# When the sums of exponentials, the roundings and the totals are issued in an attention stage with heads of 64

## The chip, the cores and the metric

The kernel runs on one core of one Trainium2 chip. The metric is the device time of one execution in microseconds (us); the time given for a kernel is the median of its runs. The core has engines that run side by side, each through its own instructions in a fixed order: PE (matrix products), DVE (vector), ACT (scalar functions), POOL (a second, slower vector engine) and SP, which here only issues DMAs. An instruction that waits holds back everything behind it on its own engine.

## The reference, cut to what matters

The program is a chain of twelve layers on a sequence of 2048 tokens of width 128: four groups, each of a feed-forward layer, an attention and the feed-forward layer again. The change touches the last attention alone (16 heads of 64, rotary embedding, causal):

```
q = rope(x @ wq.T)                      # 16 heads of 64
latent = x @ w_kv_down.T                # 64 wide
k, v = rope(latent @ w_k_up.T), latent @ w_v_up.T
scores = q @ k.T / sqrt(64) + causal
probs = softmax(scores)                 # float32
x = x + (probs @ v, heads joined) @ wo.T
```

## The kernel before

One Python function records the twelve stages. A scheduler then orders the recorded instructions on each engine: PE instructions wrapped in `pe(...)` keep the order in which they were recorded; on DVE, ACT, POOL and SP an instruction is placed when, by the scheduler's own model, its inputs are ready and its engine is free, and the recorded order decides between those that are ready together.

The last attention works on pairs of heads (64 rows of PE each, so that two matmuls run side by side) and on blocks of 512 queries: 8 pairs times 4 blocks make 32 items. `flash` records two streams that are interleaved by a planned share of columns.

- Stream A (`stream_a`) computes rough scores with queries on the rows (line 1069) and their row maxima on DVE (`mp`, line 1087, 294 of them in the stage). The maxima of an item become a third operand of the exact scores (`put_max`, lines 1959 to 1972).
- Stream B (`stream_b`) goes through an item in units: one unit is 128 keys by up to 512 queries for both heads. It records the exact scores (line 1167, eight matmuls, plus a mask at line 1020 on the diagonal), the two exponentials (ACT, line 1175, out tile `pt`) and, directly behind each exponential, `on_exp`. Then the unit is handed over as `pend`, and its value products (`values()`, line 1132) are recorded after the scores and exponentials of the next unit. `pt` has six buffers, two per unit.
- `on_exp` (line 1993) adds the exponentials into `sum`, one tile for each head. The first unit of an item is kept and added together with the second (or copied at line 1984 where the item has only diagonal units). Additions alternate between DVE and POOL; the last two units of an item are on DVE.
- `finish` runs after an item's last value product. It plans a chain with the planner's clock (`after(delay, ...)`, in ns of PE columns): `total` (column sums on PE, line 2006, copied by ACT at line 2010, sent by DMA at lines 2014 and 2016), `inverse` (reciprocal, line 2026, DMAs at 2027 and 2029), `scaled` (`ov` at line 2036), `out_b` (output product at line 2042, added to `x` on DVE at line 2045).
- Beside both streams, `fill` issues pieces of the projections of later items. `half` computes one half of a rotated query or key block (PE lines 227 to 229 or 1736 and 1737; DVE line 1772, tile `rot`), `whole` adds the halves on POOL (line 1782), and `high`, which is put into `timed` to be called LATER ns on, rounds the sum to a high part on ACT (`h`, line 1787), takes the low part on POOL (line 1788) and sends both to DRAM (lines 1789 and 1790). `rot0` has two buffers. Line 1841 loads queries and keys back, up to four items ahead.

The small PSUM tiles `s2` (three buffers) are shared by the exact scores and by `rot`, `pm`, `sums`, `py` and `v`; a score matmul can start only when an earlier user of its bank has been read.

Of the kernel before, what the change touches and what calls it, by code (L numbers as in the profile page):

```python
# [64 lines left out]
def tile_macaron(ctx: ExitStack, tc: tile.TileContext, a: dict, out: bass.AP, stages=STAGES):  # L65
# [591 lines left out]
    LATER = ((0, -60, -200, -300), (0, -40, -80, -120))  # L657
# [312 lines left out]
    def flash(io, pool, early, its, nh, causal, scale, s1, s2, pv_mm, put_max, begin, finish, poll=None,  # L970
              on_exp=None, split_at=1, fill=None, leads=None, hook=None, flush=True, order=None):
# [5 lines left out]
        halved = nh == 2  # L977
        clock = [0.0]
        total = [0]
# [13 lines left out]
        def pe(ins):  # L993
            return tc.keep_in_program_order(ins)
# [109 lines left out]
        def stream_b():  # L1104
            pend = [None]

            def values(half=None):

                if pend[0] is None:
                    return  # L1110
                n, kt, nt, c0, pts, pv, last_exp = pend[0]

                whole = not tiled or kt == 0 or CH - c0 <= CH // 2
                if half is None:
                    lo, hi = (c0 if pend_half[0] == 0 else CH // 2), CH
                elif whole:
                    lo, hi = (c0, CH) if half == 0 else (CH, CH)
                else:
                    lo, hi = (c0, CH // 2) if half == 0 else (CH // 2, CH)
                pend_half[0] = 0  # L1120
                if half == 0:
                    pend_half[0] = 1
                    if hi == CH:
                        pend[0] = None
                        pend_half[0] = 0
                else:
                    pend[0] = None
                for j in reversed(range(nh)):
                    if lo == hi:
                        break  # L1130
                    lhsT, out_rows = pv_mm(n, j, kt)
                    i = pe(nc.tensor.matmul(  # L1132
                        pv[out_rows, lo:hi], lhsT, pts[j][:, lo:hi], start=kt == 0, stop=kt == nt - 1 and hi == CH
                    ))
                    if j == nh - 1:

                        tc.add_manual_dep(
                            i.ins, last_exp.ins.name,
                            mybir.DependencyInfo(
                                mybir.DependencyClass.Sync, mybir.DependencyReason.DATA  # L1140
                            ),
                            reason="together",
                        )
                step((hi - lo) * 4)
                if kt == nt - 1 and hi == CH:
                    finish(n, pv, after, pe)

            pend_half = [0]

            for n, (g, qc) in enumerate(its):  # L1150
                while n not in ready:
                    yield 0
                at[0], at[1] = n, 0
                nt = chunks(qc) * TC
                pv = None
                for kt in range(nt):
                    at[1] = kt
                    c0 = CH - width(kt, qc)
                    diag = causal and kt >= qc * TC
                    pts = {}  # L1160
                    if halved:
                        outs = [bank("s2"), bank("s2")]
                        terms = [s2(n, j, kt) for j in range(2)]
                        for i in range(len(terms[0])):
                            for j in range(2):
                                lhsT, rhs = terms[j][i]
                                pe(nc.tensor.matmul(  # L1167
                                    outs[j][:, c0:], lhsT, rhs[:, c0:],
                                    start=i == 0, stop=i == len(terms[0]) - 1 and not diag,
                                ))  # L1170
                        if diag:
                            half_masks([ps[:, c0 : c0 + P] for ps in outs], "maskk")
                        for j in range(2):
                            pts[j] = early.tile([P, CH], F32, name="pt", tag="pt", bufs=2 * nh + 2)
                            ex = nc.scalar.activation(pts[j][:, c0:], outs[j][:, c0:], AF.Exp, scale=scale)  # L1175
                            if on_exp is not None:
                                on_exp(n, kt, j, pts, c0)
                        step((CH - c0) * (len(terms[0]) - 2))
                        yield 2 * (CH - c0)
                        values()  # L1180
                    for at_j, j in enumerate(() if halved else order):
                        if alive[0] or at_j % 2:
                            ps = bank("s2")
                        else:
                            ps = first_pass_bank()[:, :CH]
                        terms = s2(n, j, kt)
                        for i, (lhsT, rhs) in enumerate(terms):
                            pe(nc.tensor.matmul(  # L1188
                                ps[:, c0:], lhsT, rhs[:, c0:],
                                start=i == 0, stop=i == len(terms) - 1 and (tiled or not diag),  # L1190
                            ))
                        if diag and not tiled:
                            pe(nc.tensor.matmul(
                                ps[:, c0 : c0 + P], masks_b["ident_b"], masks_b["maskk_b"], start=False, stop=True
                            ))
                        pt = early.tile([P, CH], F32, name="pt", tag="pt", bufs=2 * nh + 2)
                        ex = nc.scalar.activation(pt[:, c0:], ps[:, c0:], AF.Exp, scale=scale)  # L1197
                        if diag and tiled:
                            ex = nc.gpsimd.affine_select(
                                pt[:, c0 : c0 + P], pt[:, c0 : c0 + P], [[1, P]], ALU.is_ge, 0.0,  # L1200
                                base=0, channel_multiplier=-1,
                            )
                        pts[j] = pt
                        if on_exp is not None:
                            on_exp(n, kt, j, pts, c0)
                        if len(terms) > 1:
                            step((CH - c0) * (len(terms) - 1))
                        yield CH - c0
                        if tiled and alive[0]:
                            if at_j % 2:  # L1210
                                values(at_j // 2)
                        elif at_j == (split_at if alive[0] else nh - 1):
                            values()
                    if pv is None:
                        pv = held("pv")
                    pend[0] = (n, kt, nt, c0, pts, pv, ex)
                    if not alive[0]:
                        io.lead(2.3)
                if poll is not None:
                    at[1] = nt  # L1220
                    if flush and n + 1 < len(its) and its[n + 1][0] != g:
                        values()
                    poll(at)
            values()
# [475 lines left out]
    def attn3(io, k, w, early):  # L1700
        D = L3D
        NP = L3H // 2
        NK, NQ, NV = 6, 5, 5
        SPACE, AHEAD, LATER, SHARE = 1300.0, 12, 3500.0, 2
        RC, OUT = 5000.0, 8000.0
        wdn, raw = w
        xT, lat = [None] * NC, [None] * NC
# [42 lines left out]
        pieces, pieces_v, timed = [], [], []  # L1750
# [3 lines left out]
        def make(m):  # L1754
            p, c = its[m]
            halves = {}

            def half(what, i):
                if what == "q" and i == 0:
                    halves["tabs"] = tabs_of.pop()  # L1760
                    if c == 0:
                        weights(p)
                wh, wl = pw[p]
                o = (2 * (what == "k") + i) * P
                w = tuple(t[:, o : o + P] for t in (wh, wl))
                ps = bank("rot")
                if what == "q":
                    product(ps, w, xT[c])
                else:
                    latents(ps, w, lat[c], False)  # L1770
                t = scratch(F32R, f"rot{i}")
                nc.vector.tensor_tensor(t.bitcast(F32), ps, halves["tabs"][i], ALU.mult)  # L1772
                halves[i] = t
                if i == 1:
                    if what == "k":
                        tabs_of.append(tables(scratch, "l3rope", (c + 1) % NC))
                    whole(what)
# [36 lines left out]
        with tc.tile_pool(name="att0", bufs=1) as pool0, tc.tile_pool(name="att", bufs=1) as pool:  # L1814
# [182 lines left out]
            def finish(n, pv, after, pe):  # L1997
# [41 lines left out]
                def out_b():  # L2039
# [6 lines left out]
                    if p == NP - 1:  # L2046
                        io.mark(qc)

                after(2500.0, total)

            flash(io, pool, pool, its, 2, True, 0.125, s1, s2, pv_mm, put_max, begin, finish, watch,
                  on_exp, split_at=1, fill=fill, leads=leads)
# [241 lines left out]
```

## Time and profile before

| what | value |
|---|---|
| median of 3 runs | 3780.92 us (3779.64 to 3800.57) |
| the profiled execution's own time | 3787.8 us |
| its span, first to last instruction | 3786.1 us |
| stretch of the last attention | about 2700 to 3640 us of the span |
| PE busy in the span | 3471.8 us |
| additions of exponentials in the stage (line 1993), DVE | 338 |
| the same on POOL | 218 |
| roundings in the stage (line 1787, ACT) | 52, 619 ns each |
| totals in the stage (line 2006, PE) | 124 records, 612 ns each |

The profile comes from one execution. "Busy" is the union of an engine's instruction records; the records of PE overlap, since matmuls are pipelined and pairs run side by side. "A <- B" in a list of waits says that engine and line A sat idle until B was done.

### The profile page before, as it was taken

The numbers are of one execution on the slowest core, as the hardware profiler recorded it, in microseconds if no ns is written. First come the engines' busy times: TensorE is split into PE (matmuls) and PEld (weight loads), VectorE is DVE, ScalarE is ACT, GpSimd is POOL, SyncE is SP. The second block draws the span as 40 slices with busy tenths as digits, with TensorE's granted clock in tenths as the row PEclk, the third lists the DMA queues.
The fourth block names the chain that finished last, engine by engine and source line by source line (L and its number), as shares of the span: only waits on it lengthen the run. The fifth ranks groups of instructions, "written<-read, shape, count | busy, mean of one in ns | idle before, by whom it ended". The sixth has DMA issues, their size and how long they took to land. (4 is left out here: it accounts for less than half of the span.)

```text
span 3786.1 us, 64819 instructions
## 1 busy us (share of the span) xinstructions
PE 3471.8 (92%) x25405; PEld 1858.4 (49%) x25405; DVE 2866.0 (76%) x4795; ACT 2049.4 (54%) x3858; POOL 833.8 (22%) x834
## 2 busy tenths in 40 slices
PE   7689988979999999996999999988899999999989
PEld 5543356853333333783333333366444444445457
DVE  6588556667999997668799999654767776777862
ACT  3246822315888888322688888732334444444442
POOL 1511123010000000112000000142555444533341
PEclk9779989975999999996799999899899999999999
DMA  3410123000000000102000000012443232211010
GB/s 104 94 50 17 39 60 88 1 26 5 14 10 14 8 3 1 35 1 70 8 15 6 16 6 4 7 53 75 149 140 113 92 108 96 92 63 49 24 34 12
DMA packets 124115, 170.47 MB, mean 45 GB/s; under 512 B 24032, under 2 KB 51938, under 8 KB 123808
## 3 DMA queue, kind: packets, MB, share of 16 engines
q1 hardware_dynamic: 121248, 161.07, 13.6%
q0 software_dynamic: 2560, 5.25, 0.9%
q8 instruction: 200, 3.28, 0.4%
q14 instruction: 107, 0.88, 0.1%
HBM read 101.51 MB, written 45.87 MB: 39 GB/s over the span
## 5 line engine op out<-in xcount | busy, mean ns | idle before, releaser
L1087 DVE TENSOR_REDUCE mp<-s 128x2 f32<-128x1024 f32 (+3 forms) x1440 | 1628.5, 1183 | 111.6 <-PE s L1069 69.6
L1197 ACT ACTIVATE pt<-s 128x512 f32<-128x512 f32 (+1 forms) x2368 | 1220.9, 602 | 256.7 <-PE s L1188 157.7
L1132 PE MATMUL pv<-pt,v 128*32 128x256 f32 (+5 forms) x9848 | 1068.6, 445 | 23.0 <-ACT ov L1566 10.9
L1188 PE MATMUL s<-q,km 32*128 32x512 f32 (+2 forms) x2368 | 753.3, 508 | 23.5 <-ACT pt L1197 13.7
L1069 PE MATMUL s<-km,qt 32*128 32x512 f32 (+3 forms) x2368 | 638.4, 522 | 57.3 <-DVE mp L1087 35.9
L1188 PEld LDWEIGHTS s<-q,km 32*128 32x128 f32 (+1 forms) x2368 | 330.4, 190 | 553.2 <-issue 358.8
L1175 ACT ACTIVATE pt<-s 128x512 f32<-128x512 f32 (+3 forms) x640 | 306.1, 530 | 381.9 <-PE s L1167 237.8
L1132 PEld LDWEIGHTS pv<-pt,v 128*32 128x32 f32 (+1 forms) x9848 | 236.1, 113 | 401.2 <-issue 208.0
L143 POOL TENSOR_TENSOR rs<-rs,minus_half 128x4 f32<-128x4 f32 x56 | 57.4, 1025 | 1562.1 <-DVE rs L142 1561.3
L1993 DVE TENSOR_TENSOR sum<-sum,pt 128x512 f32<-128x512 f32 (+3 forms) x328 | 260.4, 811 | 104.9 <-ACT pt L1175 103.0
L1993 POOL TENSOR_TENSOR sum<-sum,pt 128x512 f32<-128x512 f32 (+1 forms) x200 | 268.2, 1341 | 208.0 <-ACT pt L1175 204.7
L1167 PE MATMUL s<-q,k 64*128 64x512 f32 (+3 forms) x1920 | 299.5, 404 | 14.7 <-ACT pt L1175 9.8
L1069 PEld LDWEIGHTS s<-km,qt 32*128 32x128 f32 (+1 forms) x2368 | 242.5, 196 | 119.4 <-DVE mp L1087 79.2
L1167 PEld LDWEIGHTS s<-q,k 64*128 64x128 f32 x1920 | 161.8, 188 | 209.1 <-issue 122.1
L715 ACT ACTIVATE sg<-pg 128x1024 f32<-128x1024 f32 x72 | 73.9, 1027 | 174.3 <-PE pg L229 158.8
L1069 PE MATMUL s<-k,q 64*128 64x512 f32 (+3 forms) x640 | 135.0, 434 | 13.1 <-DVE mp L1087 12.3
L725 PEld LDWEIGHTS pd<-l1d,h 128*128 128x128 f32 x1152 | 139.3, 192 | 5.6
L725 PE MATMUL pd<-l1d,h 128*128 128x128 f32 x1152 | 140.1, 275 | 0.0
L1772 DVE TENSOR_TENSOR rot<-rot,tab 128x512 f32<-128x512 f32 x128 | 87.7, 686 | 62.5 <-PE rot L229 32.0
L717 DVE TENSOR_TENSOR h<-pu,sg 128x1024 f32<-128x1024 f32 x72 | 87.9, 1221 | 60.5 <-PE pu L229 55.4
L1167 PE MATMUL s<-q,two 64*128 64x512 f32 (+3 forms) x640 | 128.8, 370 | 0.0
L1782 POOL TENSOR_TENSOR rot<-rot,rot 128x512 f32<-128x512 f32 x64 | 88.6, 1385 | 160.5 <-DVE rot L1772 125.7
(573 smaller groups left out, 4585.7 us busy)
## 6 DMA issues: line engine op xcount, KB each, us to landing
tab<-in_l3rope SPq DMA_DIRECT2D x66, 256.0 KB
q<-q SPq DMA_DIRECT2D x32, 512.0 KB
k<-k SPq DMA_DIRECT2D x32, 512.0 KB
l0e<-in_l0e SPq DMA_DIRECT2D x32, 256.0 KB
q<-h SPq DMA_DIRECT2D x32, 256.0 KB
q<-rot SPq DMA_DIRECT2D x32, 256.0 KB
k<-h SPq DMA_DIRECT2D x32, 256.0 KB
k<-rot SPq DMA_DIRECT2D x32, 256.0 KB
```

The lines of the kernel that those rows point to most:

```text
L717: nc.vector.tensor_tensor(h.rearrange("p m n -> p (m n)"), pu, sg, ALU.mult)
L725: nc.tensor.matmul(pd[:, i, :], h[:, m, i * P : (i + 1) * P], wd[:, m, :], start=m == 0, stop=m == 1,)
L1069: pe(nc.tensor.matmul(ps[:, o : o + w], lhsT, rhs[:, :w], start=True, stop=not masked))
L1087: ins = nc.vector.tensor_reduce(mp[:, r, j0 : j0 + 2, kc], both[:, :, :w], AX.X, ALU.max,)
L1132: i = pe(nc.tensor.matmul(pv[out_rows, lo:hi], lhsT, pts[j][:, lo:hi], start=kt == 0, stop=kt == nt - 1 and hi == CH))
L1167: pe(nc.tensor.matmul(outs[j][:, c0:], lhsT, rhs[:, c0:], start=i == 0, stop=i == len(terms[0]) - 1 and not diag,))
L1175: ex = nc.scalar.activation(pts[j][:, c0:], outs[j][:, c0:], AF.Exp, scale=scale)
L1188: pe(nc.tensor.matmul(ps[:, c0:], lhsT, rhs[:, c0:], start=i == 0, stop=i == len(terms) - 1 and (tiled or not diag),))
L1197: ex = nc.scalar.activation(pt[:, c0:], ps[:, c0:], AF.Exp, scale=scale)
L1772: nc.vector.tensor_tensor(t.bitcast(F32), ps, halves["tabs"][i], ALU.mult)
L1782: nc.gpsimd.tensor_tensor(f, f, halves[1].bitcast(F32), ALU.add)
L1993: eng.tensor_tensor(t[:, c0:], other[:, c0:], pts[j][:, c0:], ALU.add)
```

## The change

Three things are altered, all for the attention with heads of 64.

The two `on_exp` calls of a unit leave the place directly behind its exponentials and are recorded at the head of `values()`, ahead of the unit's value products. They thus come after the scores and exponentials of the next unit. `high` is planned 9000 ns after `whole` instead of 3500, and `half` now calls waiting `high`s first when more than one is waiting at the start of a new rotated tile. `total` is planned 4000 ns after an item's last value product instead of 2500.

```diff
@@ values(), in stream_b
                 n, kt, nt, c0, pts, pv, last_exp = pend[0]
+                if halved:
+
+                    for j in range(2):
+                        on_exp(n, kt, j, pts, c0)
@@ stream_b
                             ex = nc.scalar.activation(pts[j][:, c0:], outs[j][:, c0:], AF.Exp, scale=scale)
-                            if on_exp is not None:
-                                on_exp(n, kt, j, pts, c0)
                         step((CH - c0) * (len(terms[0]) - 2))
@@ attn3
-        SPACE, AHEAD, LATER, SHARE = 1300.0, 12, 3500.0, 2
+        SPACE, AHEAD, LATER, SHARE = 1300.0, 12, 9000.0, 2
@@ make(m)
             def half(what, i):
+                while i == 0 and len(timed) > 1:
+                    timed.pop(0)[1]()
@@ finish
-                after(2500.0, total)
+                after(4000.0, total)
```

No instruction is added or removed.

## The prediction

> **What bounds the kernel now.** I read the page first: engine shares, the busy tenths and the chain.
>
> ```profile
> PE 3471.8 (92%) x25405; PEld 1858.4 (49%) x25405; DVE 2866.0 (76%) x4795; ACT 2049.4 (54%) x3858; POOL 833.8 (22%) x834
> ...
> PE   7689988979999999996999999988899999999989
> ...
> PE 13%; DVE 2%; issue 1%; DMA 1%; POOL 1%; ACT 0%; SPq 0%; POOLq 0%; ACTq 0%; DVEq 0%
> PE s L1167 4%; PE pv L1132 3%; PE s L1069 1%; PE bank L228 1%; PE bank L229 1%; PE bank L227 1%; DVE mp L1087 1%; PE py L2042 0%; PE s L1020 0%; PE bank L922 0%; DVE sum L1993 0%; ACT pt L1175 0%; PE sums L2006 0%; DMA sum<-inv 0%; DMA inv<-rc 0%
> ```
>
> PE is at 9 tenths nearly everywhere, and the chain runs mostly through PE. The change touches only the stage from about 2700 to 3640 us, so the second view is busy time by stretch (stretch, length, busy time per engine with instruction counts, granted clock, DMA share, GB/s):
>
> ```profile
> 2700.00:3640.00 940.00, 899.57 (x6070) 449.20 (x6070) 711.39 (x1033) 402.50 (x812) 444.36 (x334) 0.98 0.26 85
> ```
>
> PE is idle for 940.0 - 899.6 = 40.4 us there. Third, the waits of that stretch (us in total, times, longest): of PE, then of DVE and of ACT.
>
> ```profile
> PE s L1167 <- ACT pt L1175: 9.8, 9, 2.0
> PE s L1069 <- DVE mp L1087: 9.7, 16, 1.3
> PE pm L1967 <- DVE rot L1772: 5.6, 4, 2.9
> PE rot L229 <- POOL pwL L222: 3.6, 2, 2.8
> PE s L1167 <- DVE x L2045: 3.1, 3, 1.8
> ...
> PE sums L2006 <- DVE rot L1772: 1.2, 3, 0.4
> PE sums L2006 <- DVE sum L1993: 0.9, 1, 0.9
> ```
>
> ```profile
> DVE sum L1993 <- ACT pt L1175: 105.3, 104, 3.4
> ```
>
> ```profile
> ACT h L1787 <- POOL rot L1782: 114.1, 51, 4.4
> ```
>
> The two queues that the change aims at do stall (105 us in DVE behind an addition that waits for its exponential, 114 us in ACT behind a rounding that waits for POOL), but PE sees little of it: 9.7 us for maxima, 9.8 us for exponentials. Those stalls lie beside PE work. Fourth, one stretch of the timeline, to see such a stall reach PE:
>
> ```profile
> 3133.97 1.27 POOL L1993 TENSOR_TENSOR sum<-sum,pt 128x512 f32<-128x512 f32 x1 [3.04 <-ACT pt L1175]
> 3134.35 1.44 DVE L1993 TENSOR_TENSOR sum<-sum,pt 128x512 f32<-128x512 f32 x1
> ...
> 3135.71 1.21 DVE L1087 TENSOR_REDUCE mp<-s 128x2 f32<-128x1024 f32 x1
> ...
> 3136.98 0.50 PE L1069 MATMUL s<-k,q 64*128 64x512 f32 x2 [0.57 <-DVE mp L1087]
> ```
>
> The maximum starts when the addition ends, and PE waits 0.57 us for its bank.
>
> **The change part by part.** No work is added, so the cost is all in order. I compared the order of the built programs engine by engine, which the diff alone does not tell. Nothing differs ahead of the last attention. In it, the scheduler had already placed most instructions when their inputs are ready, so few move.
>
> *Additions a unit on.* Of 352 additions on DVE, 30 stand later by one or two maxima and 8 stand earlier; of the stage's 294 maxima 38 have one addition fewer ahead, 16 one more. On POOL six or seven of 224 stand behind a low part (L1788) that they stood ahead of. Gain: at most all 9.7 us of PE <- mp. Measured as the start of each late matmul less the usual step between such a pair, 26 waits for maxima stand in the stage, and ten of them (5.0 us) have a moved addition ahead of the maximum; I take 3 us of these. Loss: 16 maxima with an addition more ahead, 0.68 us each (the unblocked 128x512 addition), 11 us if PE felt all of it; 26 of 294 maxima were felt, so 16 x 26/294 x 0.68 = 1 us. Net -2, ends -10 and +11.
> The rotated halves (DVE L1772) in front of pm, sums and rot made PE wait 5.6 + 1.2 + 1.4 = 8.2 us; five of these waits (4.8 us) have an addition fewer ahead. I take half: -2, ends -5 and 0.
>
> *A rule against taking PE's idle time as the cap.* The row says PE busy 96% of the stage. The Trainium skill ("Perfetto Trace Analysis", Identifying the Most-Contended Engine) says that matmul busy time does not show distance to the roofline and that weight-load busy share is the better measure; here that is 449.2 of 940 us, 48%. By the rule there is headroom beyond 40 us; by the row it is all of 40 us. I go with the waits: the gaps inside the busy time are put down to "issue" (119.5 us ahead of score weights alone), which no moved addition shortens. The sum by the rule would let the gain be larger but names no wait that this change removes.
>
> *A rule that prices the addition itself.* The addition at 3134.35 took 1.44 us beside a POOL addition that ran to 3135.24, while one at 3133.36 without it took 0.68. The skill ("SBUF — State Buffer", Who interferes with whom) says that a DVE instruction with two SBUF inputs and a GpSimd instruction that reads SBUF exclude each other, and that a tensor_reduce never takes part. By the rule each of the 30 additions put behind a maximum saves up to 1.44 - 0.68 = 0.76 us of DVE, 23 us in all; by the rows DVE is busy 711 of 940 us and not the bound, so I count only what PE waited for, as above. The rule also speaks against the change: an addition put off meets POOL's L1782 and L1788, which read SBUF too, so the lock may only move.
>
> *Roundings later.* In ACT's order 58 of 64 roundings stand where they stood and six stand one unit *earlier*, ahead of two exponentials. The planned delay thus hardly takes effect. A rounding that waits for POOL holds the exponentials behind it; at 2784.23 one that had waited 4.26 us made PE wait 1.49 us. Six of these would be +9 us; below nothing is not excluded, since POOL's moved additions no longer stand ahead of L1788 there: -2. I take +2. Their DMAs (L1789, L1790) keep their place among the loads on SP but for one; the loads run items ahead, and no PE wait of the stage is for a DMA. Without that lead a load would cost what SP now waits behind it (L1789 up to 10.7 us).
>
> *Totals 1500 ns on.* 62 of 64 total matmuls and nearly all 128 output matmuls go one unit later on PE, same durations. The waits of PE sums (1.2 + 0.9 = 2.1 us) can go. The bank of py is freed by the addition to x (0.68 us); in the built program 57 score matmuls wait on DVE instead of 43. Before, 3 of 43 were felt, 3.1 us: 14 x 3.1/43 = +1, at most 14 x 0.68 = +9.5. On SP seven or eight inverse DMAs (L2014, L2016) go behind one load of queries or keys; `inverse` and `scaled` follow 5000 and 8000 ns on, and what is late next is `ov` (16.5 us of DVE waits, 14 times), then py. On ACT 15 copies of sums go behind one more unit's exponentials, which lets those come sooner. Value -1, ends -2 and +9.5.
>
> *Buffers of exponentials.* An addition must end before the exponential three units on reuses its buffer. From the timeline, the time left has a median of 6.6 us on DVE and 6.8 on POOL, but for the kept first units it falls to 0.15. If every addition ran a unit (940/320 = 2.9 us) later, 13 units would be short, 20.7 us in all. About 45 of 576 move: 20.7 x 45/576 = +1.6, ends 0 and +20.7; I take +1.
>
> Sum: -2 - 2 + 2 - 1 + 1 = -2 us. Against the profiled execution's own time (3786.1 us of span, 1.7 us around it, 3787.8) this is 3785.8. That execution lies 6.9 us over the median of the runs shown, so I forecast 3780.9 - 2 = 3779 us.
>
> **The rivals.**
>
> *The recorded order means nothing.* The scheduler's readiness, not the planned delays, sets the order; 58 of 64 roundings speak for it, the 62 moved totals and the 38 maxima against it. It gives 3781.
>
> *The waits go.* DVE's maxima and ACT's exponentials come free, and beside them the waits for pm, sums and x: 9.7 + 9.8 + 5.6 + 2.1 + 3.1 = 30 us, 3751 us. For it: those queues stall 105 and 114 us. Against it: the roundings do not move, and nine waits of 0.7 to 1.5 us for maxima have the same additions ahead as before. All 40 us of idle time would give 3741.
>
> *Slower: the buffers of exponentials run out.* Place: ACT at line 1175 waiting for additions of the unit three back, in front of PE's scores. In the trace ACT waited once, 1.4 us, for that. A shift by a whole unit costs 20.7 us (3802), by 4 us 46.6 us (3828). It decides from a shift of about 3.7 us, where it passes 1% (38 us). Against it: POOL's and DVE's built orders move by one place in a few per cent of cases.
>
> **How the numbers follow.** A measurement of this kernel tells about 1% (38 us) from no change. Forecast (3779, its own ends 3765 to 3795): 62%. Order means nothing: 15%. Waits go: 9%, of which 2 are past 1%. Buffers run out: 14%, of which 6 are past 1%. Range 3760 to 3803: it holds the first two, part of the third, and the fourth at one unit's shift. Faster by over 1% 0.02, within 0.92, slower 0.06.
>
> **What would show it right or wrong.** PE <- mp near 7 to 9 us and PE idle in the stage near 38 us would bear the sum out. The mean of the 128x512 addition on DVE (1125 ns) should fall a little; if it falls towards 682 ns the lock part was undersized. ACT <- h should stay over 100 us; if it falls far below, the roundings did move. ACT pt waiting for sums by more than 10 us is the slow rival. A change outside the last attention, or a granted clock in it other than 0.98, would make the sum wrong whatever the waits do.

## The result: 0.4% slower, nearly all of it idle time of PE in the last attention

| | before | after |
|---|---|---|
| median of 13 runs each, same chip | 3786.84 us (3779.64 to 3800.57) | 3799.78 us (3790.5 to 3810.6) |
| profiled execution, its own time | 3787.8 us | 3804.16 us |
| span | 3786.1 us | 3802.4 us |

The ratio after to before is 1.0039, 95% interval 1.0026 to 1.0052: 3786.84 x 0.0039 = 15 us slower (10 to 20; the two medians lie 12.9 us apart). The forecast was 2 us faster than a median of 3780.92 us from three runs; with thirteen runs that median is 3786.84. The measured time lies inside the range that was given, but the change has the other sign, and the interval leaves zero out.

Where did it go? The first part of the page of after says what did not change: every engine's busy time is within 4 us of before.

```profile
PE 3472.6 (91%) x25405; PEld 1861.6 (49%) x25405; DVE 2869.7 (75%) x4795; ACT 2049.9 (54%) x3858; POOL 833.3 (22%) x834
```

So the engines do the same work and wait more. To find the place, the last attention is cut at the same two points of the work in both kernels (from 12 us ahead of its first exponential to 3 us behind its last). First before, then after; columns as in the prediction: stretch, length, busy time of PE, PE's weight loads, DVE, ACT and POOL with counts, granted clock, DMA share, GB/s.

```profile
2648.80:3640.50 991.70, 944.56 (x6344) 472.53 (x6344) 752.83 (x1092) 423.55 (x853) 469.09 (x353) 0.97 0.27 89
```

```profile
2650.20:3656.00 1005.80, 944.61 (x6344) 475.77 (x6344) 755.38 (x1092) 423.77 (x853) 468.32 (x353) 0.97 0.27 87
```

The stage is 14.1 us longer, of 16.3 us for the span. PE's busy time in it is the same to 0.05 us, and the granted clock is the same to two digits. PE's idle time went from 991.7 - 944.6 = 47.1 us to 61.2 us, and that is the whole difference of the stage. (The 40.4 us of the prediction are for 2700 to 3640 us; this cut starts 51 us sooner.) The waits of PE in this stretch of after (us in total, times, longest) say what it waited for:

```profile
PE s L1069 <- DVE mp L1087: 20.0, 27, 4.0
PE s L1171 <- ACT pt L1179: 12.7, 17, 2.0
PE pm L1971 <- DVE rot L1776: 6.3, 4, 3.1
PE s L1171 <- DVE x L2049: 3.8, 3, 1.5
PE py L2046 <- ACT q L1976: 3.2, 6, 0.5
PE rot L229 <- POOL pwL L222: 2.6, 3, 1.6
PE rot L1738 <- DVE x L2049: 2.2, 2, 1.6
```

The same waits in the same cut of before:

```profile
PE s L1069 <- DVE mp L1087: 11.2, 19, 1.3
PE s L1167 <- ACT pt L1175: 9.8, 9, 2.0
PE pm L1967 <- DVE rot L1772: 6.6, 5, 2.9
PE rot L229 <- POOL pwL L222: 3.6, 2, 2.8
PE s L1167 <- DVE x L2045: 3.1, 3, 1.8
...
PE rot L1736 <- DVE x L2045: 0.3, 1, 0.3
```

The output product (`py`) never waited for `q` there. The rises are 8.8 (maxima) + 2.9 (exponentials) + 3.2 (`py`) + 1.9 (`rot`) + 0.7 (scores behind `x`) = 17.5 us; three waits fell by 5.0 us together (`sums` behind rotated halves, `rot` behind reciprocals, and `rot` behind POOL's low parts of weights). That leaves 12.5 of the 14.1 us. One wait is new and large, 4.00 us for a maximum; the rest are many small ones that grew.

What stood ahead of these maxima on DVE can be read from the traces. Where an addition of exponentials ran directly ahead of the maximum, PE's waits add up to 10.7 us in 13 in after and 3.9 us in 7 in before. None of these maxima stands directly behind an addition to `x`.

The queues that the change aimed at, in the same cut of after: DVE's additions, then ACT's roundings and exponentials.

```profile
DVE sum L1997 <- ACT pt L1179: 109.4, 97, 3.4
...
DVE ov L2040 <- DMA sum<-inv: 21.8, 16, 4.8
```

```profile
ACT h L1791 <- POOL rot L1786: 155.8, 57, 13.3
...
ACT pt L1179 <- POOL sum L1997: 5.6, 1, 5.6
```

Neither stall went away: additions wait 109 us as they did (108.9 in this cut of before), roundings 156 us instead of 131. The second line of each pair belongs to the longest single stall of after, here in the timeline (start, duration, engine, line, operation; in brackets the idle time before it and what ended it):

```profile
3111.48 0.28 PE L1020 MATMUL s<-halfmaskk,halfident 64*128 64x128 bf16 x4
3112.74 0.69 DVE L2040 TENSOR_TENSOR ov<-ov,sum 128x512 f32<-128x512 f32 x1 [4.83 <-DMA sum<-inv]
...
3113.56 1.26 POOL L1997 TENSOR_TENSOR sum<-pt 128x512 f32<-128x512 f32 x1 [9.34 <-DVE ov L2040]
...
3114.86 1.09 ACT L1179 ACTIVATE pt<-s 128x512 f32<-128x512 f32 x2 [5.59 <-POOL sum L1997]
...
3115.30 1.01 DVE L1087 TENSOR_REDUCE mp<-s 128x2 f32<-128x256 f32 x2
3115.76 0.69 PE L1069 MATMUL s<-k,q 64*128 64x384 f32 x2 [4.00 <-DVE mp L1087]
```

Read it from the top down. DVE waits at `ov` for the inverses to come back from DRAM, 4.83 us. The tile that `ov` reads frees the next item's first addition on POOL, that one frees an exponential's buffer, and the maximum behind `ov` on DVE frees PE's bank: PE stands for 4.00 us. It shows how far a single late DMA reached here, but it is one stall of 4 us in a loss of 14; the experiments tell whether a loss of this size needs it.

### The profile page after: what moved, and what is told of

It reads as the page before. It is cut to its first block, busy times and chain, and to the rows that moved or that the text cites. A ratio compares the mean times of both kernels' runs of the same rounds, so it can differ in the third digit from the quotient of the medians.

```text
span 3802.4 us, 64814 instructions
## 1 busy us (share of the span) xinstructions
PE 3472.6 (91%) x25405; PEld 1861.6 (49%) x25405; DVE 2869.7 (75%) x4795; ACT 2049.9 (54%) x3858; POOL 833.3 (22%) x834
## 5 line engine op out<-in xcount | busy, mean ns | idle before, releaser
L1136 PE MATMUL pv<-pt,v 128*32 128x256 f32 (+5 forms) x9848 | 1068.3, 445 | 22.5 <-ACT ov L1568 10.8
L1171 PE MATMUL s<-q,k 64*128 64x512 f32 (+3 forms) x1920 | 301.5, 404 | 18.3 <-ACT pt L1179 12.7
L1791 ACT CAST h<-rot 128x512 fp32r<-128x512 f32 x64 | 39.6, 619 | 169.2 <-POOL rot L1786 169.2
```

What stands on the lines that cost most here:

```text
L1136: i = pe(nc.tensor.matmul(pv[out_rows, lo:hi], lhsT, pts[j][:, lo:hi], start=kt == 0, stop=kt == nt - 1 and hi == CH))
L1171: pe(nc.tensor.matmul(outs[j][:, c0:], lhsT, rhs[:, c0:], start=i == 0, stop=i == len(terms[0]) - 1 and not diag,))
```

## The experiments

The theories. The first: the totals carry the loss, because with `total` the whole chain behind it (inverse, `ov`, output product, addition to `x`) moves, and PE meets other neighbours. The second: the additions carry it, by being in front of other maxima on DVE. A third, for the way in which the totals could cost: inverses come late, `ov` holds DVE (the timeline above), and more buffers would cure it. All ratios are to runs of before on the same chip in the same round, with 95% intervals; the median of before differs from round to round (3786.61, 3790.19, 3787.20 and 3799.13 us), so absolute times of different rounds can't be compared. Stage lengths and waits are from the profiled execution, cut as above, and idle is the stage's length less PE's busy time. The profiled execution is a single run, and its time can lie far from the median: 13 us above it in `t2_after_out_back`, 12 us below it in `v1_late_s1` and `v3_after_s1`.

### Each of the three edits alone

`e1_total`: before with the totals edit alone.

```diff
-                after(2500.0, total)
+                after(4000.0, total)
```

> The kernel before with the total planned at 4000 instead of 2500 and nothing else. If the total's delay is the cause, nearly all of the loss is here: 3794 to 3802 us against 3787 for before, PE <- mp near 18 us and DVE ov waiting for the inverses near 22 us. If the additions are the cause: 3783 to 3791, PE <- mp near 10 us. If the loss is spread over the parts: 3790 to 3795.

Measured: 3804.56 us, 1.0048 (1.0033 to 1.0062). Stage 1007.6 us with PE idle 62.8. PE's waits begin as after's do:

```profile
PE s L1069 <- DVE mp L1087: 20.0, 28, 3.3
PE s L1167 <- ACT pt L1175: 12.6, 17, 2.0
...
PE py L2042 <- ACT q L1972: 3.2, 6, 0.5
```

`ov` waits 21.8 us for the inverses, as in after. The main waits and the loss are those of after, although this edit does not touch the additions of exponentials.

`e2_sums`: before with the additions moved alone.

```diff
+                if halved:
+                    for j in range(2):
+                        on_exp(n, kt, j, pts, c0)
...
-                            if on_exp is not None:
-                                on_exp(n, kt, j, pts, c0)
```

> The kernel before with the additions of exponentials issued with the value products a unit on and nothing else; in the built program some 25 of 1100 DVE instructions of the stage stand elsewhere and none on PE. If the total's delay is the cause: within 4 us of before (3783 to 3791). If the additions are the cause (buffers of exponentials held longer): 3794 to 3802 with ACT pt waiting for sums by 5 us or more. If spread: 3790 to 3795.

Measured: 3787.7 us, 1.0005 (0.9985 to 1.0025). Stage 992.2 us, idle 46.3, maxima 10.8 us in 18 waits (11.2 in 19 before). In the built order PE is the same as before; about 25 instructions of DVE and a few of ACT, POOL and SP stand elsewhere, and PE's idle time is within 1 us of before.

`e3_round`: before with the roundings edit alone.

```diff
-        SPACE, AHEAD, LATER, SHARE = 1300.0, 12, 3500.0, 2
+        SPACE, AHEAD, LATER, SHARE = 1300.0, 12, 9000.0, 2
...
+                while i == 0 and len(timed) > 1:
+                    timed.pop(0)[1]()
```

> The kernel before with the rounding planned at 9000 instead of 3500, and the loop in half, and nothing else. The built program has the same order on all five engines as before, so every theory expects no change, 3783 to 3791 us, ratio within 0.2% of 1; a larger difference would say how far two runs of one order lie apart.

Measured: 3788.02 us, 0.9997 (0.998 to 1.0014). The built order is that of before on all five engines (in the traces DVE, ACT, POOL and SP run their instructions in the same order throughout): this edit issues nothing later. The run therefore also shows what the measurement makes of two equal programs, up to 0.2% either way.

So one line of the change holds the loss, and the other two are without effect that could be measured.

### Which member of the chain

`total` starts a chain in which every step is planned from the one before. The next runs move one link at a time.

`s1_total_only`: `total` 1500 ns later, but `inverse`, `ov` and the output product kept at their old clock.

```diff
-        RC, OUT = 5000.0, 8000.0
+        RC, OUT = 3500.0, 8000.0
...
-                after(2500.0, total)
+                after(4000.0, total)
```

> The kernel before with the total planned at 4000 and the delay behind it cut from 5000 to 3500, so that reciprocal, ov and output product are planned at their old clock. If the loss comes from ov standing in DVE's queue before its inverses have landed (total and first DMAs later, ov where it was), it is as large or larger: 3799 to 3808 us, DVE ov waiting 22 us or more. If the loss comes from where the output product and the addition to x fall on PE and in the banks, it is gone: 3783 to 3791.

Measured: 3791.67 us, 1.001 (0.9995 to 1.0025). Stage 999.6 us in a profiled execution with a granted clock of 0.966 there (before: 0.974), PE idle 52.5, maxima 15.8 us in 23 waits.

`s2_chain_only`: `total` at its old place, the chain behind it 1500 ns later.

```diff
-        RC, OUT = 5000.0, 8000.0
+        RC, OUT = 6500.0, 8000.0
```

> The other half: the total stays at 2500 and the delay behind it grows from 5000 to 6500, so that the inverses get 1.5 us more before ov is asked for and the output product falls where it falls after the change. If ov waiting for its inverses is the cause: not slower, 3778 to 3789 us, DVE ov waiting under 12 us. If the place of the output product is the cause: 3797 to 3808.

Measured: 3802.68 us, 1.0036 (1.0008 to 1.0064). Stage 1008.8 us, idle 61.8; `py` for `q` 3.2 us in 6 again, scores behind `x` 5.1, `sums` behind `x` 6.1 in 4. `ov` waited 17.5 us for its inverses, against 16.7 in before. So most of the loss is not in `total` itself but in what follows it, and it comes with hardly any longer wait for inverses.

`t1_out_late`: of the chain, only the output product and its addition to `x` are later.

```diff
                 def scaled():
...
-                    after(1500.0, out_b)
+                    after(3000.0, out_b)
```

> The kernel before with only the output product planned 1500 ns later (3000 instead of 1500 behind ov); total, reciprocal and ov keep their clock. If the place of the output product on PE is the cause of the loss: 3798 to 3810 us against 3790 for before, ratio 1.002 to 1.006, PE py waiting for ACT q by about 3 us as in the changed kernel. If the reciprocal's or ov's place is the cause: within 0.1% of before.

Measured: 3805.67 us, 1.0041 (1.0028 to 1.0054). Its stage is 1009.3 us, PE busy 947.6, idle 61.7. PE's waits:

```profile
PE s L1069 <- DVE mp L1087: 12.7, 23, 1.9
PE s L1167 <- ACT pt L1175: 11.0, 12, 2.0
PE sums L2006 <- DVE x L2045: 7.8, 5, 1.6
...
PE s L1167 <- DVE x L2045: 4.0, 3, 1.5
...
PE py L2042 <- ACT q L1972: 3.2, 6, 0.5
...
PE rot L1736 <- DVE x L2045: 1.5, 1, 1.5
...
PE py L2042 <- DVE rot L1772: 0.9, 3, 0.3
```

Four matmuls per item (128 in the stage), moved alone, cost as much as the whole change. The wait of `py` for `q` is that of after to the digit, and there is a new one: `sums` behind the addition to `x`. Here the two sides of the product's bank account for the loss. What waits for the addition to `x` rose from 3.4 to 13.3 us, and what the product itself waits for from 0.5 to 4.1: 13.5 of the 14.6 us by which PE's idle time grew. In after the same two rose by only 2.6 and 3.7 us, and maxima rose by 8.8 us instead of 1.5. The two losses are of one size but are made up of different waits, so this run does not show by itself that after's loss is the product's. It does show that a loss of this size needs no 4 us stall: no wait for maxima is longer than 1.9 us. In PE's order the product of an item now stands directly behind a matmul of scores (exact or rough) or their mask 23 times and behind value products 8 times; in before it is 15 and 16, and in after 23 and 8 as well.

`t2_after_out_back`: after, with the output product 1500 ns nearer to `ov`, about at its old clock.

```diff
-                    after(1500.0, out_b)
+                    after(0.0, out_b)
```

> The changed kernel, all edits in, with the output product planned 0 instead of 1500 ns behind ov, so that it stands at its old clock. If the output product's place is the cause, the loss goes although total, additions and roundings are all as changed: ratio 1.000 to 1.002 to the kernel before. If late totals or moved additions carry a part: 1.003 to 1.005.

Measured: 3793.22 us, 1.0019 (1.0009 to 1.0028). About half of after's loss comes back (the two intervals just overlap), so in after too the product's place carries a part of it. The profile (stage 1005.6 us at a clock of 0.962, idle 55.8) is of the slowest of this kernel's runs. PE's order is near to that of before but not the same: the product stands behind scores or their mask 14 times, behind value products 15 times. The rest of the loss is not assigned.

### Is it lateness?

`t3_out_early`: before with the output product 1500 ns earlier (the same edit on before).

> The kernel before with the output product planned 0 instead of 1500 ns behind ov. If lateness of the output product is what costs, this gains: ratio 0.996 to 0.999. If only its place among its neighbours counts (which bank it takes, what waits for the addition to x), either sign, 0.998 to 1.004, and PE waits for DVE x tell which.

Measured: 3807.59 us, 1.0064 (1.0041 to 1.0087). Stage 1014.7 us at a clock of 0.961, idle 59.0; scores behind `x` 9.0 us in 9 waits instead of 3.1 in 3, `py` behind rotated halves 4.9, longest 4.0. Earlier loses too, and more than either expectation allowed. About half of it in this profile is waits (11.9 of the 23.0 us by which the stage is longer); the other half is busy time of PE, 955.7 us instead of 944.6, at the lower clock.

`e5_tot1000`: before with `total` 1500 ns earlier.

```diff
-                after(2500.0, total)
+                after(1000.0, total)
```

> The kernel before with the total planned at 1000 instead of 2500. If a later total costs because the whole chain behind it (copy, DMAs, reciprocal, ov, output product) is late, an earlier one gains: 3772 to 3782 us, DVE ov waiting for the inverses under 12 us. If it is only where the chain's DVE and PE instructions happen to fall, either sign is possible, within 10 us of 3787. If PE waits for the last additions in front of the total (sums <- sum), it is slower: PE sums waits 2 us before, 10 us or more here.

Measured: 3795.93 us, 1.0025 (1.0009 to 1.0042). Stage 1003.3 us, idle 56.6, maxima 19.4 us in 22 waits, scores behind `x` 4.8. Both directions lose, so what is paid for is not only a late result but a place among other neighbours: of the three values tried for each of the two delays, that of before is the best.

### Do more buffers cure it?

`s3_buffers`: after with three buffers for `sum`, `ov` and `rc` instead of two, and four DRAM tiles for inverses.

```diff
-            inv = [dram.tile([2, CH], F32, name=f"inv{i}") for i in range(2)]
+            inv = [dram.tile([2, CH], F32, name=f"inv{i}") for i in range(4)]
...
-                ov = pool.tile([P, CH], F32, name="ov", tag="ov", bufs=2)
+                ov = pool.tile([P, CH], F32, name="ov", tag="ov", bufs=3)
```

> The changed kernel with a third buffer for sum, ov and rc and four instead of two inverses in DRAM; PE's order is that of the changed kernel. If the loss is in POOL's and ACT's wait for a sum tile that ov has not yet released (9.3 us of POOL and 5.6 us of ACT at 3113), 4 to 6 us come back: 3793 to 3797. If it is only DVE standing behind ov, nothing comes back: 3798 to 3805.

Measured: 3799.94 us, 1.0024 (1.0008 to 1.0039), with PE's order that of after. Stage 1003.6 us, idle 56.7, maxima 17.6 us. ACT no longer waits for an addition (5.6 us in after), while `ov` still waits 23.7 us for inverses.

`s4_ov_late`: the same buffers, and `ov` 3000 ns later, so that its inverses have more time.

```diff
-        RC, OUT = 5000.0, 8000.0
+        RC, OUT = 5000.0, 11000.0
```

> The changed kernel with the same buffers and ov planned 11000 instead of 8000 behind the reciprocal. If DVE standing behind ov for the inverses is the main cause, most of the loss comes back: 3785 to 3792 us, DVE ov waiting under 12 us. If the scheduler leaves ov where it stood, or the loss lies elsewhere: 3797 to 3806.

Measured: 3796.61 us, 1.0026 (1.001 to 1.0041). `ov` still waited 20.1 us for inverses (21.8 in after), so this run, which puts the output product later too, did not do what it was made for. Buffers may give back a third of the loss; the intervals of both runs overlap with that of after, and it stays open. They do not cure it.

### Is it the shared small bank?

The output product takes one of the three small PSUM tiles that scores, `pm`, `sums` and `rot` share. Three kernels give it a large tile, that of the rough scores, instead: t1 so changed, before so changed, and after so changed.

```diff
-                    ps = bank("py").rearrange("p (i c) -> p i c", i=TC)
+                    ps = banks("py")[:, :CH].rearrange("p (i c) -> p i c", i=TC)
```

> The kernel before with the output product planned 1500 ns later and, besides, with its result in one of the two large PSUM buffers of the rough scores instead of one of the three small ones. If the late product costs because its small bank is wanted by the next total or score before x has been added (PE <- DVE x 13 us in the run with the late product alone) or is still held by the copy of the maxima (3 us), the loss shrinks by half or more: ratio to before 1.000 to 1.002. If it costs by its place among the rest, it stays: 1.003 to 1.006.

> The kernel before with the output product's result in a large PSUM buffer and nothing else: the control, and a candidate for a faster kernel. If the small banks are short here too (PE <- DVE x 3.4 us), 0.997 to 0.9995. If taking a buffer from the rough scores makes those wait for their maxima, 1.001 to 1.004, with PE s <- mp above 14 us.

> The changed kernel with the output product's result in a large PSUM buffer. If the shared small bank is the cause of the change's loss: 1.000 to 1.002 to the kernel before; if the place alone is: 1.003 to 1.006.

Measured: v1 3840.05 us, 1.0116 (1.0096 to 1.0135); v2 3800.66 us, 1.0011 (0.9996 to 1.0027); v3 3820.54 us, 1.0052 (1.0033 to 1.0071). The waits for `x` and `q` did leave the small banks. But in v1 the waits for maxima are 35.1 us in 34 (12.7 in t1) and the stage is 1021.7 us with 69.0 idle; in v3 they are 26.0 us in 29 (20.0 in 27 in after). The product now holds a tile that the rough scores want. In before's place the other tile costs nothing that could be measured; in the late place of t1 it almost trebles the loss, more than either expectation allowed; in after the loss is not clearly larger. So the late product loses with either tile. What the small bank by itself contributes these runs do not tell: the large tile brings waits of its own, and with it some 20 to 25 of DVE's instructions stand elsewhere in v1 and v3 (in v2, compared with before, none).

### Is it the clock?

Runs of one and the same kernel differ with the granted clock. The 63 runs of before in the round of s1 lie between 3766 and 3814 us, at mean clocks of 0.942 down to 0.926, and each 0.001 of clock goes with about 2.8 us. So part of a difference between two kernels could be clock. An estimate from the runs on record (in each round, straight lines of one slope through the runs of both kernels) puts the difference to before at equal clock at 14 us for e1 (19 between the plain means), 18 for t1 and s2 (17 and 14), 13 for t3 (21), 33 for v1 (42), 15 for v3 (19), 6 for s3, 4 to 5 for t2, s4 and e5, 2 for s1, and within 1 for e2, e3 and v2. The loss of the late chain and of the late product thus stands at equal clock too; a good third of t3's is tied to it. For after this can't be worked out, since the clocks of its thirteen runs of before are not on record. A lower clock may in turn come from more waits, so the estimate does not separate the two as causes.

No version ran faster than before.

## Why the prediction was wrong

*Totals 1500 ns on: the step that failed.* It was put at -1 us with ends at -2 and +9.5. By `e1_total` it is 3786.8 x 0.0048 = +18 us (12 to 23), beyond the upper end. The prediction saw the move ("62 of 64 total matmuls and nearly all 128 output matmuls go one unit later on PE, same durations") and costed the bank of `py` by its one known reader, the addition to `x`, at +1: scores behind `x` did rise by only 0.7 us and `rot` behind `x` by 1.9. Put at nothing were two terms. One is the other side of the bank, what the product itself finds in it: `py` waits 0.5 us in before and 4.2 in after, 3.2 of them for `q`. The other is the order on DVE behind the moved chain: maxima rise from 11.2 to 20.0 us in after and in `e1_total` alike, 6.8 us of it in waits with an addition of exponentials directly ahead of the maximum, although `e1_total` does not touch the additions. With `total` alone later (s1) maxima are at 15.8 us already. What brings those additions in front of the maxima is not shown. With the product alone moved (t1) the bank's own reader was under-priced as well: waits for the addition to `x` rose by 9.9 us, against +1 forecast. "What is late next is `ov`" was right as a statement (16.7 to 21.8 us) and was given no price; in after it stands at the head of the 4 us stall, and by s2 and t1 a loss of this size comes without that stall.

*The +9.5 was not a bound.* It counted 14 more waits of one kind, behind the addition to `x`. In after the loss was mostly of other kinds: maxima, exponentials, and the product's own wait.

*Additions: right.* -2 with ends -10 and +11; `e2_sums` gives 0.05%, about 2 us, from 6 faster to 9 slower. The 3 us of maxima that were to go did not (11.2 to 10.8).

*Rotated halves: the waits fell, the time did not.* The 2 us were to come from `pm`, `sums` and `rot` behind rotated halves. In `e2_sums` these fell by 4.3 us (6.6 to 4.6, 2.6 to 1.7, 1.4 to 0), but other waits rose (exponentials 9.8 to 11.1, `sums` behind an exponential 0 to 2.3), and PE's idle time fell by 0.8.

*Roundings: right that they hardly move, wrong by 2 us in price.* `e3_round` builds the order of before. That 58 of 64 stood still was read from the build of the whole change; that this edit alone moves none, not even the six, only its own build would have told.

*Buffers of exponentials: right in not being the mechanism.* ACT waited for an addition of the unit three back once, 5.6 us (1.4 us before), under the 10 us named for that rival; and that one came from a late `ov`, not from a late addition.

*The rivals.* "The waits go" failed: the two queues stall as before or longer (109 and 156 us). "The recorded order means nothing" holds for two of the three edits. The loss is a case that the rivals did not name: the slower one was looked for in the additions, the largest edit by lines, and it lay in the smallest. That the measured time falls inside the range is luck: the range was wide enough for a rival (buffers, one unit's shift) that did not happen. And 38 us was taken for what a measurement tells from no change; the runs told 15.

*The measures.* PE's idle time in the stage was the right one: it was to fall to 38 us and rose by 14.1, which is the result. The share of weight loads (48%), which the prediction weighed and set aside, names no wait that moved: PE's busy time in the stage stayed at 944.6 us while the time moved, so setting it aside was right for this change; the rule itself no run here tests. The addition's mean on DVE (128x512, two inputs) fell a little, as forecast, from 1125 to 1114 ns, far from 682, so little came of the lock part:

```profile
L1997 DVE TENSOR_TENSOR sum<-sum,pt 128x512 f32<-128x512 f32 x160 | 178.2, 1114 | 66.9 <-ACT pt L1179 66.8
```

*How it could have been seen.* The built order was compared for the change as a whole. Built one by one, the edits would have shown ahead of any run that the roundings change nothing, that the additions leave PE as it was, and that all PE moves are the totals'. A forecast of about zero for two edits and an open sign for the third would have followed.

*What stays open.* Which line holds the loss is shown, and that moving the product alone costs as much. How after's 15 us divide between the product's place, the total's and the changed order on DVE is not: t2 gives back about half. Open too is the 0.1 to 0.2% by which s1 and t2 still stand over before, at the edge of what these runs resolve.

## What to carry to other kernels

Build each edit by itself and compare its instruction order on each engine before costing it: a delay that the scheduler overrides costs nothing, and the shortest line may hold all the moves. On a stage where PE is busy 95% of the time, price a moved PE instruction on both sides of its bank (who must leave, who comes next), and look for what else changes order with it on the other engines; give such a move an open sign, wider than the waits it touches, for around a tuned place both directions lost here (0.4% later, 0.6% earlier).

## What the runs showed of the hardware

Some short waits of PE come with a lower granted clock, which adds to them. In the windows of after around the 4 us stall (columns as above; the clock is the third figure from the end):

```profile
3104.00:3110.00 6.00, 6.00 (x44) 2.78 (x42) 3.87 (x5) 2.76 (x5) 0.22 (x1) 1.00 0.24 79
3110.00:3116.00 6.00, 2.00 (x18) 1.03 (x14) 3.26 (x5) 1.09 (x2) 2.36 (x2) 0.89 0.34 71
3116.00:3122.00 6.00, 6.00 (x32) 2.81 (x32) 3.61 (x10) 0.78 (x2) 3.19 (x4) 0.54 0.21 57
3122.00:3128.00 6.00, 6.00 (x52) 3.22 (x52) 5.87 (x8) 2.86 (x8) 3.56 (x3) 1.00 0.39 131
```

In the slice behind the stall PE is busy throughout, but the clock is 0.54 and 32 matmuls get through where 44 and 52 do in the slices with 1.00. The price can be read off the same work in before, where PE does not wait at this place and the clock is 1.00. From the rough score that the stall held up to the next rough score but one, first before, then after (value products in between):

```profile
3103.15 0.42 PE L1069 MATMUL s<-k,q 64*128 64x384 f32 x2
...
3104.04 1.08 PE L1132 MATMUL pv<-pt,v 128*64 128x512 f32 x4
...
3106.74 0.50 PE L1069 MATMUL s<-k,q 64*128 64x512 f32 x2
```

```profile
3115.76 0.69 PE L1069 MATMUL s<-k,q 64*128 64x384 f32 x2 [4.00 <-DVE mp L1087]
...
3117.39 1.98 PE L1136 MATMUL pv<-pt,v 128*64 128x512 f32 x4
...
3121.95 0.50 PE L1069 MATMUL s<-k,q 64*128 64x512 f32 x2
```

That is 3.59 us in before and 6.19 in after, 2.60 us more. The wait of 4 us thus cost two thirds more than the waits view says, in this one instance. It is not so for every wait: after's last attention has ten waits of PE over 1.5 us, and behind five of them (one of 2.06 us) the clock in the next 3.4 us is 1.00; behind the other five it is between 0.50 and 0.57. Nor is it what made the kernel slower: the mean clock of the stage is 0.97 in both.
